# Row sums in a symmetric attention kernel: four of twelve steps folded aside instead of eight, and reductions allowed only in steps that turn nothing

## The chip, the cores and the metric

The kernel runs on one core of a Trainium2 chip. Its time is the device time of one execution in microseconds. TensorE (PE in the profile) multiplies matrices, VectorE (DVE), ScalarE (ACT) and GpSimd (POOL) work on tiles of 128 partitions, and SyncE (SP) issues most of the DMA transfers. Each engine has its own list of instructions, and semaphores make one engine wait for another.

## The reference, cut to what matters

The network has several layers on four images of 128 channels and 64x64 positions. The change touches one part of layer 2 only, attention in which queries, keys and values are all the same tensor `q`, with 16 heads of 8 numbers over L = 4096 positions:

```
qkv = _qz_ring(heads + rx_theta)
q = jnp.transpose(qkv, (0, 2, 1, 3))
scores = jnp.einsum('bhsd,bhtd->bhst', q, q) / np.sqrt(D)
attn = jax.nn.softmax(scores, axis=-1)
ctx = jnp.einsum('bhst,bhtd->bhsd', attn, q)
```

(The reference reshapes the four images of 4096 positions as its batch.) Queries and keys are the same, so the matrix of scores is symmetric: exp of the score of query s with key t is also that of query t with key s. The softmax is computed as a sum of exp times value, the numerator, divided by a sum of exp, the denominator.

## The kernel before

**Tiles.** For one head the 4096 queries are cut in four blocks `j` = 0 to 3 of 1024, and the keys in sixteen tiles `m` = 0 to 15 of 256. A step of the loop in line 1103 is one (head `h`, block `j`, key tile `m`). It makes 256 x 1024 scores on TensorE (lines 1119 to 1126, tile `score`), their exp on ScalarE in two instructions (line 1142, `p` = 0 and 1, tile `ex`, four buffers), and multiplies exp by values on TensorE into `ctx_ps` one step later (`weigh`, line 1041).

**Symmetry.** The kernel makes only the scores with `m // 4 >= j`. A step with `m // 4 > j` (the code calls it `behind`) is used a second time: VectorE turns its two halves into the tile `turned`, the first half in the same step (line 1148) and the second in the next step (line 1129, through `upright`). Four such steps fill one `turned` tile. Some steps later TensorE multiplies it by values into `acc_ps` (`turn`, line 995, eight turns a group), and VectorE copies or adds the finished group into `acc` (lines 1021 and 1023). Steps with `m // 4 == j` turn nothing.

**Row sums.** The denominator of the turned side is the sum of each row of `ex` over its 1024 queries. It is made in one of two ways, as `folded(j, m)` (line 1083) says:

- ScalarE accumulates it while it makes the exp (`accum_out` in line 1143), two instructions with an accumulator read each;
- or the step is "aside": GpSimd folds `ex` in two additions, 128x2048 values to 128x1024 (line 1090, `folded`) and to 128x512 (line 1091, `quarters`, six buffers), and VectorE reduces the quarters to two columns of `dacc` (line 1135). Line 1092 puts the reduction on the list `folds` with the step from which it is due.

**Order.** `pairs(j)` (line 968) gives the order of the key tiles in a block, and line 977 the blocks: block 0 of head h, block 3 of head h-1, block 1 and block 2 of head h. From head to head 40 steps repeat. I number them as places 0 to 39. Place by place the key tiles are

```
block 0, places  0-15: 4 5 6 0  7 8 9 1  10 11 12 2  13 14 15 3
block 3, places 16-19: 12 13 14 15      (of the head before)
block 1, places 20-31: 8 9 4  10 11 5  12 13 6  14 15 7
block 2, places 32-39: 12 8  13 9  14 10  15 11
```

and the steps that turn nothing are places 3, 7, 11, 15 to 19, 22, 25, 28, 31, 33, 35, 37 and 39. The lists of TensorE, VectorE and GpSimd stand in this order as written (`manual_schedule`, line 1256). Within a step VectorE's list is: the copy of a group that the step's turns have finished; the second transposition of the step before; the copy of `ctx_ps` at the end of a block (line 1072); the reductions that are due; the first transposition of this step. TensorE's list is: scores, turns (line 1127), `ctx_ps` products of the step before. A group may be turned from two steps after its last step on (`begun[...] < n - 1`).

With j = 0, 1, 2 the steps aside are, before the change, 8 of 12, 4 of 8 and 3 of 4, so 15 for each head.

Of the kernel before, what the change touches and what calls it, by code (L numbers as in the profile page):

```python
# [29 lines left out]
class Common:  # L30
# [57 lines left out]
    def mm(self, out, lhsT, rhs, start=True, stop=True):  # L88
        self.nc.tensor.matmul(out, lhsT, rhs, start=start, stop=stop)  # L89
# [685 lines left out]
def layer2_attention(K, xd, dpool, w):  # L775
# [6 lines left out]
    with ExitStack() as ctx:  # L782
# [126 lines left out]
        def attention(qt, dsum, big, work, pssc, psctx, psacc):  # L909
# [11 lines left out]
            def load(h, queues=(nc.sync, nc.sync)):  # L921

                out = []
                for keys in (True, False):
                    t = work.tile([P, L // 2], F32R, name="keys" if keys else "queries")
                    raw = t.bitcast(F32)
                    n = P if keys else CH
                    for p in range(2):  # L930
                        for c in range(2):
                            for k in range(4):
                                r = unit(p, c).start + HD * k
                                src = head_d[k // 2 if keys else k % 2, HD * h : HD * h + HD]
                                at = p if keys else c
                                queues[not keys].dma_start(  # L936
                                    out=raw[r : r + HD].rearrange("d (m s) -> d m s", s=n),
                                    in_=src.rearrange("d (m z s) -> d m z s", z=2, s=n)[:, :, at],
                                )
                    out.append(t)  # L940
                return out

            def rounded(t):

                nc.gpsimd.tensor_copy(t, t.bitcast(F32))  # L945
# [12 lines left out]
            def spread_values(v):  # L958
                t = work.tile([P, 4 * BT, 4, HD], F32, name="turned_v")
                nc.gpsimd.tensor_tensor(  # L960
                    t,
                    v.unsqueeze(2).to_broadcast([P, 4 * BT, 4, HD]),
                    quarter.unsqueeze(1).to_broadcast([P, 4 * BT, 4, HD]),
                    ALU.mult,
                )
                return t
# [63 lines left out]
            def turns(n, ready):  # L1030


                due = left = 0
                for g in groups:
                    left += BT - g[0]
                    due = max(due, -(-left // max(1, g[5] - n + 1)))
                for _ in range(min(max(due, 1), 3)):
                    if not groups or not ready(groups[0]) or turn():
                        return
# [41 lines left out]
            folds = []  # L1081

            def folded(j, m):

                return ((m - 4) % 3 < 2, m % 2 == 0, m % 4 < 3)[j]

            def fold(n, exs, at):
                hs = work.tile([P, 2, CH], F32, name="folded", bufs=1)
                qs = work.tile([P, 2, CH // 2], F32, name="quarters", bufs=6)
                nc.gpsimd.tensor_tensor(hs, exs[:, :, 0], exs[:, :, 1], ALU.add)  # L1090
                nc.gpsimd.tensor_tensor(qs, hs[:, :, 0 : CH // 2], hs[:, :, CH // 2 :], ALU.add)  # L1091
                folds.append((n + 5, qs, at))

# [7 lines left out]
            for n, (h, j, m) in enumerate(steps):  # L1103
                now[0] = n
                keys, queries = heads[h]
                if j in (1, 2) and h + 1 < NH:
                    at = n - begins[h, 1]
                    if at == 0:
                        heads[h + 1] = load(h + 1)
                    if at in (11, 15):  # L1110
                        rounded(heads[h + 1][at == 15])
                while waiting and n >= waiting[0][0]:
                    _, at, v = waiting.pop(0)
                    values[at] = spread_values(v)
                behind = m // 4 > j
                if n in ends:
                    turned = work.tile([P, BT, 2 * CH], F32, name="turned")
                    end = min(ends[n], last[h, m // 4])
                sps = [pssc.tile([P, 2, CH], F32, name="score") for p in range(2)]
                for p in range(2):  # L1120
                    for c in range(2):
                        mm(
                            sps[p][:, c, :],
                            keys[unit(p, c), m * P : (m + 1) * P],
                            queries[unit(p, c), j * CH : (j + 1) * CH],
                        )
                turns(n, lambda g: begun[id(g[4])] < n - 1)
                if upright is not None:
                    nc.vector.transpose(*upright)  # L1129
                    upright = None  # L1130
                if past is not None:
                    weigh(*past)
                while folds and folds[0][0] <= n:
                    _, qs, at = folds.pop(0)
                    nc.vector.tensor_reduce(at, qs, AX.X, ALU.add)  # L1135
                exs = work.tile([P, 2, 2, CH], F32, name="ex", bufs=4)
                aside = behind and folded(j, m)
                for p in range(2):
                    ex = exs[:, p]
                    t = 2 * m + p  # L1140
                    summed = behind and not aside
                    nc.scalar.activation(  # L1142
                        ex, sps[p], AF.Exp, scale=scale, accum_out=dacc[:, j, h, t : t + 1] if summed else None
                    )
                    if behind:
                        upright = turned[:, t % BT, :], ex.rearrange("p c s -> p (c s)")
                        if p == 0:
                            nc.vector.transpose(*upright)  # L1148
                if aside:
                    fold(n, exs, dacc[:, j, h, 2 * m : 2 * m + 2])  # L1150
                past = (h, j, m, exs)
                if behind and m % 4 == 3:
                    begun[id(turned)] = n
                    groups.append([0, h, j, m // 4, turned, end, None])
# [82 lines left out]
        for b in range(NB + 1):  # L1237
            with tc.tile_pool(name="l2_big", bufs=1) as big:
                with (
                    tc.tile_pool(name="l2_mid", bufs=2) as work,  # L1240
                    tc.tile_pool(name="l2_ps", bufs=8, space=PSUM) as psum,
                ):
                    parts = [feed_forward(b - 1, past, work, psum)] if b > 0 else []
                    if b < NB:
                        part, qt = prepare(b, big, work, psum)
                        parts.append(part)
                    run(*parts)
                if b == NB:
                    break
                past = keep.tile([P, NTT, NH], F32, name="dsum")  # L1250
                with (
                    tc.tile_pool(name="l2_work", bufs=2) as work,
                    tc.tile_pool(name="l2_pssc", bufs=3, space=PSUM) as pssc,
                    tc.tile_pool(name="l2_psctx", bufs=1, space=PSUM) as psctx,
                    tc.tile_pool(name="l2_psacc", bufs=1, space=PSUM) as psacc,
                    tc.manual_schedule(
                        engines={mybir.EngineType.PE, mybir.EngineType.DVE, mybir.EngineType.Pool}
                    ),
                ):
                    attention(qt, past, big, work, pssc, psctx, psacc)  # L1260
# [433 lines left out]
```

## Time and profile before

| what | value |
|---|---|
| runs, median (lowest to highest) | 11169.24 us (11165.61 to 11181.6) |
| profiled execution, its own time | 11175.99 us |
| its span on the core | 11174.1 us |
| attention, four images | 1369.6, 1370.4, 1367.5, 1370.3 us |
| one head inside an image (40 steps) | 85.3 us |
| PE, DVE, ACT, POOL busy over the span | 81%, 70%, 66%, 55% |
| exp, L1142 | 5120 of 1.031 us |
| first transposition, L1148 | 1536 of 1.232 us |
| second transposition, L1129 | 1536 of 1.208 us |
| reduction of quarters, L1135 | 960 of 0.648 us |
| fold and second fold, L1090 and L1091 | 960 of 2.387 us and 960 of 1.285 us |
| accumulator read of exp, L1142 | 1152 of 0.208 us |

Times are those of one profiled execution. A timeline has one row for each instruction or run of like instructions: its start in us from the start of the span, its length, engine, source line, what it writes and reads, how many; in square brackets the idle time of the engine just before it and the work that ended this idle time. TensorE's matrix multiplications all have line 89 (a helper), so they are told apart by tile. Lengths of neighbours on VectorE and ScalarE overlap by some hundredths of a microsecond, so what an instruction takes from its engine is read from start to start.

### The profile page before, as it was taken

Reading aid. Unit: us, or ns where it says so; the run is one execution under the profiler, and the core shown is the slowest. Engines: PE = TensorE matmul, PEld = TensorE weight load, DVE = VectorE, ACT = ScalarE, POOL = GpSimd, SP = SyncE. Lnnn points to the kernel's source line nnn. Section 1 sums busy time; section 2 is a strip of 40 time slices with the busy share of each in tenths; the row PEclk is TensorE's granted clock in tenths of the full one; section 3 lists DMA queues with packets and bytes.
Section 4 is the critical chain, followed back from the end, with each engine's and each line's share of the span. In section 5 each row is a group of like instructions: output and inputs, shape, how many; then the busy total and the mean of one; then the engine's idle time right before and its main releaser. Section 6 shows DMA issues by size and latency. Waiting matters only on the chain.

```text
span 11174.1 us, 183363 instructions
## 1 busy us (share of the span) xinstructions
PE 9093.3 (81%) x71376; PEld 3383.0 (30%) x71376; DVE 7817.5 (70%) x8718; ACT 7349.5 (66%) x9690; POOL 6136.5 (55%) x3631
## 2 busy tenths in 40 slices
PE   5777777778757999967999967999967999966767
PEld 2222223223122333322333322333322333323433
DVE  2688687687846788856888756878856888844564
ACT  2655454654527899947988947988946998842431
POOL 0466455455626777726777736777736777720000
PEclk8787878878778999978999979999978999978888
DMA  3322322322212221122221222221122221122004
GB/s 86 83 70 52 100 64 62 92 62 61 61 46 39 34 33 34 30 73 36 37 33 32 32 74 34 38 32 33 32 73 34 35 37 33 32 87 78 30 16 136
DMA packets 524324, 581.53 MB, mean 52 GB/s; under 512 B 106232, under 2 KB 329536, under 8 KB 520896
## 3 DMA queue, kind: packets, MB, share of 16 engines
q1 hardware_dynamic: 520896, 565.61, 22.4%
q8 instruction: 563, 9.22, 0.4%
q10 hardware_dynamic: 2560, 4.20, 0.3%
q14 instruction: 305, 2.50, 0.1%
HBM read 373.96 MB, written 76.55 MB: 40 GB/s over the span
## 4 chain that ended last, share of the span: by engine, by line
PE 35%; DVE 16%; DMA 8%; SPq 4%; ACT 3%; issue 2%; POOL 1%; DVEq 0%; ACTq 0%; POOLq 0%
PE ctx_ps L89 12%; PE acc_ps L89 9%; DVE turned L1129 5%; PE score L89 5%; DVE turned L1148 5%; SPq L936 4%; DMA queries<-head_d 3%; DMA keys<-head_d 2%; PE ln_var L89 2%; PE ln_xc L89 1%; PE hid_ps L89 1%; DMA w<-in_L_ffn_weight 1%; PE ffn_ps L89 1%; ACT ex L1142 1%; PE kv L89 1%
## 5 line engine op out<-in xcount | busy, mean ns | idle before, releaser
L1142 ACT ACTIVATE ex<-score 128x1024 f32<-128x1024 f32 x5120 | 4904.7, 1031 | 598.5 <-PE score L89 224.9
L1090 POOL TENSOR_TENSOR folded<-ex 128x1024 f32<-128x1024 f32 x960 | 2291.5, 2387 | 1173.3 <-ACT ex L1142 1141.8
L89 PE MATMUL ctx_ps<-ex,qt 128*32 128x512 f32 x20480 | 2722.5, 596 | 0.0
L1148 DVE STREAM_TRANSPOSE turned<-ex 128x1024 f32<-128x1024 f32 x1536 | 1892.0, 1232 | 596.5 <-ACT ex L1142 392.8
L89 PE MATMUL acc_ps<-turned,turned_v 128*32 128x256 f32 x24576 | 1828.5, 389 | 220.7 <-DVE turned L1129 219.0
L1129 DVE STREAM_TRANSPOSE turned<-ex 128x1024 f32<-128x1024 f32 x1536 | 1854.8, 1208 | 0.0
L89 PE MATMUL score<-queries,keys 32*128 32x512 f32 x10240 | 1360.2, 497 | 240.9 <-POOL queries L945 145.9
L641 DVE TENSOR_TENSOR_SCAN hs<-decay,carry,hs 128x512 f32<-128x512 f32 x1024 | 1247.8, 1263 | 151.6 <-ACT decay L640 142.3
L640 ACT ACTIVATE decay<-dt,a_neg 128x512 f32<-128x512 f32 x1024 | 699.9, 690 | 875.1 <-DVE hs L641 871.5
L1091 POOL TENSOR_TENSOR quarters<-folded 128x512 f32<-128x512 f32 x960 | 1233.8, 1285 | 75.3
L647 POOL TENSOR_TENSOR hs<-hs,c_sb 128x1024 f32<-128x1024 f32 x512 | 1201.7, 2368 | 48.1 <-DMA c_sb<-c_d 28.4
L89 PEld LDWEIGHTS score<-queries,keys 32*128 32x128 f32 x10240 | 523.4, 182 | 2300.9 <-issue 1656.8
L89 PEld LDWEIGHTS acc_ps<-turned,turned_v 128*32 128x32 f32 x24576 | 562.1, 108 | 938.9 <-issue 545.2
L89 PE MATMUL y_ps<-hs,pair 128*64 128x512 f32 x2048 | 654.5, 757 | 223.0 <-POOL hs L647 222.8
L89 PEld LDWEIGHTS ctx_ps<-ex,qt 128*32 128x32 f32 x20480 | 684.9, 110 | 462.2 <-DVE ctx L1072 53.2
L637 DVE TENSOR_TENSOR hs<-dtx,b_ps 128x2048 f32<-128x2048 f32 x256 | 581.4, 2271 | 318.9 <-PE b_ps L89 218.2
L644 POOL COPY carry<-hs 128x4 f32<-128x4 f32 x256 | 65.1, 254 | 1105.2 <-DVE hs L641 1090.8
L1135 DVE TENSOR_REDUCE dacc<-quarters 128x2 f32<-128x512 f32 x960 | 617.2, 648 | 0.0
L1072 DVE COPY ctx<-ctx_ps 128x512 f32<-128x512 f32 x256 | 177.1, 692 | 565.3 <-PE ctx_ps L89 565.3
L89 PE MATMUL ln_var<-ln_sq,mean 128*128 128x512 f32 x448 | 289.6, 732 | 219.0 <-ACT ln_sq L104 183.1
L89 PE MATMUL b_ps<-dbc,spread 32*128 32x512 f32 x512 | 341.6, 751 | 147.8 <-DVE hs L637 147.8
L960 POOL TENSOR_TENSOR turned_v<-v,quarter 128x1024 f32<-128x1024 f32 x192 | 458.9, 2391 | 0.0
(344 smaller groups left out, 9320.8 us busy)
## 6 DMA issues: line engine op xcount, KB each, us to landing
c_sb<-c_d SPq DMA_DIRECT2D x512, 128.0 KB
keys<-head_d SPq DMA_DIRECT2D x1024, 64.0 KB
queries<-head_d SPq DMA_DIRECT2D x960, 64.0 KB
dt<-dt SPq DMA_DIRECT2D x128, 256.0 KB
dtx<-dtx SPq DMA_DIRECT2D x128, 256.0 KB
w<-in_L_ffn_weight SPq DMA_DIRECT2D x32, 1024.0 KB
w<-in_L_ffn_weight SPq DMA_DIRECT2D x128, 256.0 KB
under<-xp SPq DMA_DIRECT2D x384, 66.0 KB
```

What stands on the lines that cost most here:

```text
L89: self.nc.tensor.matmul(out, lhsT, rhs, start=start, stop=stop)
L637: nc.vector.tensor_tensor(hs, dtx2, bb.unsqueeze(1).to_broadcast([P, NQ, CH]), ALU.mult)
L640: nc.scalar.activation(ex, dt2[:, q, :], AF.Exp, scale=a_neg[:, q, g : g + 1])
L641: nc.vector.tensor_tensor_scan(hs[:, q, :], ex, hs[:, q, :], carry[:, g, q : q + 1], ALU.mult, ALU.add)
L647: nc.gpsimd.tensor_tensor(at, at, cs.unsqueeze(1).to_broadcast([P, 2, CH]), ALU.mult)
L960: nc.gpsimd.tensor_tensor(t, v.unsqueeze(2).to_broadcast([P, 4 * BT, 4, HD]), quarter.unsqueeze(1).to_broadcast([P, 4 * BT, 4, HD]), ALU.mult,
L1090: nc.gpsimd.tensor_tensor(hs, exs[:, :, 0], exs[:, :, 1], ALU.add)
L1091: nc.gpsimd.tensor_tensor(qs, hs[:, :, 0 : CH // 2], hs[:, :, CH // 2 :], ALU.add)
L1129: nc.vector.transpose(*upright)
L1135: nc.vector.tensor_reduce(at, qs, AX.X, ALU.add)
L1142: nc.scalar.activation(ex, sps[p], AF.Exp, scale=scale, accum_out=dacc[:, j, h, t : t + 1] if summed else None)
L1148: nc.vector.transpose(*upright)
```

## The change

```diff
             def folded(j, m):
 
-                return ((m - 4) % 3 < 2, m % 2 == 0, m % 4 < 3)[j]
+                return ((m - 4) % 3 == 0, m % 2 == 0, m % 4 < 3)[j]
 
             def fold(n, exs, at):
...
-                folds.append((n + 5, qs, at))
+                folds.append((n + 3, qs, at))
...
-                while folds and folds[0][0] <= n:
+
+                while folds and (folds[0][0] <= n and not behind or len(folds) > 5):
                     _, qs, at = folds.pop(0)
                     nc.vector.tensor_reduce(at, qs, AX.X, ALU.add)
```

In block 0 the key tiles 4, 7, 10 and 13 stay aside; 5, 8, 11 and 14 get their row sums from ScalarE's accumulator instead. A head has 11 steps aside instead of 15, so the kernel has 704 instead of 960. A reduction is due three steps after its fold instead of five, but is given to VectorE only in a step that turns nothing, unless more than five are waiting.

Lines from 1133 on move down by one.

## The prediction

> **What bounds the kernel now.** I first read the busy times of one image's attention as a stretch of its own, since the change touches nothing else.
>
> ```profile
> core 0: us, PE busy (x) PEld busy (x) DVE busy (x) ACT busy (x) POOL busy (x), PEclk, DMA share, GB/s
> 5087.50:6457.90 1370.40, 1302.11 (x14569) 464.15 (x14569) 1101.20 (x1167) 1230.59 (x1568) 1046.06 (x558) 1.00 0.21 32
> ```
>
> TensorE is busy 1302 of 1370 us at a granted clock of 1.00, so it is the bound, and at most its idle 68 us per image can go. ScalarE follows with 1231 us. GpSimd, which the change relieves most, has 1046 us and room. Next I asked the waits of TensorE in one head of 40 steps (head 6 of the second image, 85.3 us):
>
> ```profile
> PE acc_ps L89 <- DVE turned L1129: 3.3, 5, 1.6
> PE score L89 <- ACT ex L1142: 0.9, 1, 0.9
> ```
>
> TensorE waits 3.3 us, five times, for a second transposition (L1129), and once 0.9 us for an exp. Its timeline puts the five at places 0, 6, 11, 26 and 32, with 0.17, 0.41, 1.55, 0.67 and 0.55 us: each time the first turn of a new group. The 0.9 us comes at place 39. Heads inside an image repeat this to some hundredths. The page's groups tell what stands in VectorE's list beside transpositions:
>
> ```profile
> L89 PE MATMUL acc_ps<-turned,turned_v 128*32 128x256 f32 x24576 | 1828.5, 389 | 220.7 <-DVE turned L1129 219.0
> ...
> L1135 DVE TENSOR_REDUCE dacc<-quarters 128x2 f32<-128x512 f32 x960 | 617.2, 648 | 0.0
> ```
>
> All such waits together are 219 us; the 960 reductions are 617 us of VectorE. So the question is which reductions stand ahead of which late transposition. That is read from VectorE's timeline before the longest wait:
>
> ```profile
> 5609.76 0.64 DVE L1135 TENSOR_REDUCE dacc<-quarters 128x2 f32<-128x512 f32 x1
> 5610.32 1.23 DVE L1148 STREAM_TRANSPOSE turned<-ex 128x1024 f32<-128x1024 f32 x1
> 5611.48 1.20 DVE L1129 STREAM_TRANSPOSE turned<-ex 128x1024 f32<-128x1024 f32 x1
> 5612.61 0.64 DVE L1135 TENSOR_REDUCE dacc<-quarters 128x2 f32<-128x512 f32 x1
> 5613.17 1.23 DVE L1148 STREAM_TRANSPOSE turned<-ex 128x1024 f32<-128x1024 f32 x1
> 5614.32 1.21 DVE L1129 STREAM_TRANSPOSE turned<-ex 128x1024 f32<-128x1024 f32 x1
> 5615.78 1.25 DVE L1148 STREAM_TRANSPOSE turned<-ex 128x1024 f32<-128x1024 f32 x1 [0.25 <-ACT ex L1142]
> 5618.00 0.42 DVE L1021 COPY acc<-acc_ps 128x256 f32<-128x256 f32 x1 [0.97 <-PE acc_ps L89]
> 5618.35 1.24 DVE L1129 STREAM_TRANSPOSE turned<-ex 128x1024 f32<-128x1024 f32 x1
> 5619.50 0.64 DVE L1135 TENSOR_REDUCE dacc<-quarters 128x2 f32<-128x512 f32 x1
> 5620.07 1.23 DVE L1148 STREAM_TRANSPOSE turned<-ex 128x1024 f32<-128x1024 f32 x1
> 5621.22 1.20 DVE L1129 STREAM_TRANSPOSE turned<-ex 128x1024 f32<-128x1024 f32 x1
> ```
>
> These are the transpositions of places 5, 6, 8 and 9. The last row ends at 5622.42, and TensorE's turn starts at 5622.48:
>
> ```profile
> 5620.16 0.77 PE L89 MATMUL score<-queries,keys 32*128 32x512 f32 x4
> 5622.48 0.64 PE L89 MATMUL acc_ps<-turned,turned_v 128*32 128x256 f32 x8 [1.55 <-DVE turned L1129]
> ```
>
> Elsewhere a turn starts 0.43 us after its scores; here 2.32 us. So 1.88 us are lost, of which the profile shows 1.55 as idle. Three reductions lie in this stretch, each 0.56 us from its start to the next.
>
> **What the Trainium skill says.** Perfetto Trace Analysis, section "Tensor Engine Instruction (MATMUL, LD_WEIGHTS)", says that VectorE, ScalarE and GpSimd are strict FIFOs. The trace agrees: the copy L1021 sat 0.97 us, and the transposition behind it with it, though its exp had ended at 5616.67. VectorE: DVE Perf Modes, section "Rules for kernel authors", advises restructuring when a reduction lies on a hot path; here it costs 0.56 us for 512 values a partition. ScalarE: Activation LUTs, section "What it computes", names the accumulator output but no price; the trace gives one below.
>
> **The change part by part.**
>
> *GpSimd loses folds.* Four a head, 256 in all, of 2.387 + 1.285 us: 940 us of its work. Value: nothing. Exps that reuse an `ex` buffer wait for the fold of four places earlier (places 4, 5, 8, 9, 12, 13, 16, 17), and those folds ended 1.4 us or more ahead of them. The casts of keys and queries keep their order, and no wait of TensorE inside a head is for them.
>
> *VectorE loses 256 reductions and the rest move.* 256 x 0.56 = 143 us leave its list. Only what stands ahead of a late transposition counts, so I go through the waits with the new list: of each head's eleven reductions one stands at each of places 3, 7, 11, 15, 25, 28, 31, 33, 35, 37 and 39, behind the second transposition of the step before.
>
> - Place 6, 0.41 us. From the copy of `ctx_ps` at 5599.19 to the transposition that ends at 5609.84 VectorE never idles, and one reduction lies between (5602.08). It goes to place 39 of the head before, but that of place 0's fold comes to place 3. One for one: 0.
> - Place 11, 1.55 us. The first reduction (5609.76) goes; the transpositions behind it start up to 0.5 us earlier. The second is replaced by that of place 7. But place 8's first transposition must wait for its exp (5615.75) and the copy L1021 for TensorE (5618.00): both clocks are TensorE's, so what was gained before them is absorbed. The third (5619.50) stands after them and goes. The two transpositions behind it have their exp ready (it ended at 5618.95), so they end 0.57 us earlier, at 5621.85, and so does TensorE's wait: **0.57**.
> - Places 26 and 32, 0.67 and 0.55 us. No reduction lies between the copy of `ctx_ps` or the ScalarE-bound transposition that begins either chain and its last transposition: 0.
> - Places 39 and 0, 0.86 and 0.17 us. ScalarE's exp of place 38 is late, and in both built programs it waits for TensorE's `ctx_ps` product of place 37. Untouched: 0.
>
> What is late next at place 11 is the same transposition, 1.31 us behind instead of 1.88.
>
> The first head of each image is different, since there no block 3 lies between blocks 0 and 1 to let VectorE catch up. Its timeline shows TensorE idle 1.54 us at place 11 as above, and then 0.82 us (turn at 5125.19) and 1.26 us (5138.58). Ahead of the first stand two more reductions (5119.04, 5121.89), ahead of the second another two (5130.08, 5132.93), and none in the new list. Two are 1.13 us, less what exps that follow TensorE, now itself earlier, hold back. My walk with the rows' starts gives 0.7 and 0.65. Sum for an image: 1.35.
>
> *ScalarE gains accumulations.* Four steps a head, two instructions each, 512 in all. An exp with accumulator takes 1.00 us to the next start (5630.19 less 5629.19), one without 0.92 (a row of two is 1.94 long, one alone 1.02), and the read, 0.208 us in its own row, overlaps the next exp. Price 0.08 to 0.10 each, 41 to 51 us in all; I take 0.10. If the whole read were exposed it would be 0.208, 106 us: the upper end. The lower end is zero, since more work on a FIFO can't gain. Value on the path: 0. What places 1, 5 and 9 lose, 0.2 us each, is covered by the idle 0.41, 0.55 and 0.31 us before the exps of places 2, 7 and 10. Place 13 is tightest: the exps of place 14 start 0.2 us later against TensorE, and the second half of place 15's scores reuses the buffer of the first of them. It ended at 5629.22, the scores start at 5629.51, so 0.29 us of cover shrink to about 0.1. If that is gone, it costs up to 0.2 a head, 13 us.
>
> *The new due time.* A reduction now comes three to five steps after its fold and VectorE waits there if GpSimd isn't done, with the next block's copies and transpositions queued behind it. At place 7 the quarters were ready at 5612.38 and VectorE comes at about 5614.5. At place 39, behind the cast of queries, they end at 5680.51 and VectorE comes at 5681.93. Both are in time: 0. `len(folds) > 5` never holds.
>
> **Sum.** 64 x 0.57 = 36.5; 4 x 1.35 = 5.4; together 42 us. Against the profiled execution, 11175.99 (span 11174.1 and 1.9 around it), that is 11134. The median of the runs is 6.75 lower, 11169.24, so I predict 11127 us. About 0.2%, 22 us, is what a measurement of this kernel can tell from no change.
>
> **The rivals.**
>
> *Absorbed.* The third reduction's place is taken up too, by the copy L1021 or an exp. For it: two of three reductions in the stretch go that way already. Against it: after 5618.35 the rows follow without a gap. Time 11169, within 10.
>
> *ScalarE comes onto the path (slower).* In block 0 it has eight accumulating steps of twelve. If its backlog isn't emptied between pairs of them (places 1-2, 5-6, 9-10, 13-14), exps come late, transpositions wait for them instead of for reductions, and the 0.57 isn't had. Price 4 x 2 x 0.10 = 0.8 us a head, 51 in all: 11220. It decides from the point where the exps at place 9 come 1.6 us later (transposition at 5620.65 against their new end of about 5619.05). For it: ScalarE is second in busy time. Against it: gaps of 0.31 to 1.28 us before places 7, 8, 9, 10 and 12.
>
> *More is freed.* If place 6's chain also loses its reduction, because VectorE gets to place 3 early enough, 64 x 0.41 = 26 us more: 11101. The FIFO walk speaks against it.
>
> **How the numbers follow.** The forecast has 0.74, its own range 11112 to 11142 (up to 13 us less for the tight score, 15 more for head 0 and neighbours). Absorbed 0.12, slower 0.05, more freed 0.09. Two tenths may be left out, so the range takes part of the freed case and some shortfall: 11098 to 11152. Faster by over 0.2% is the forecast and the freed case less a little: 0.81. Within: 0.14. Slower: 0.05.
>
> **What would show it.** In the new profile TensorE's wait at place 11 should be near 1.0 us instead of 1.55, those at places 6, 26, 32, 39 and 0 as they are, a head near 84.7 us instead of 85.3, the waits on L1129 near 178 us instead of 219, and no reduction between two transpositions of steps 8 and 9. ScalarE should have 1664 accumulator reads. Wrong: idle before exps gone in block 0, or VectorE waiting for quarters.

## The result and the profile after

| what | before | after |
|---|---|---|
| runs, median | 11169.24 us | 11122.35 us |
| runs, lowest to highest | 11165.61 to 11181.6 us | 11118.96 to 11132.05 us |
| profiled execution, its own time | 11175.99 us | 11123.57 us |
| its span | 11174.1 us | 11121.7 us |
| attention, four images | 1369.6, 1370.3, 1367.5, 1370.3 us | 1357.3, 1356.5, 1356.6, 1356.6 us |
| one head inside an image | 85.30 us | 84.71 us |

The median fell by 46.9 us; the ratio of after to before is 0.9956, its interval 0.9941 to 0.997. The forecast was 42 us less. The two profiled executions lie 52.4 us apart, of which 50.7 are in the attention (5477.7 less 5427.0 us, the four images together).

First the busy times of the same stretch, one image's attention, in the profile after. The columns are those of the prediction's first fence.

```profile
core 0: us, PE busy (x) PEld busy (x) DVE busy (x) ACT busy (x) POOL busy (x), PEclk, DMA share, GB/s
5076.40:6432.90 1356.50, 1299.70 (x14568) 463.98 (x14569) 1062.13 (x1103) 1240.51 (x1696) 812.00 (x430) 1.00 0.20 33
```

GpSimd has lost 234 us of work in this image and VectorE 39, ScalarE has gained 10, and the stretch is 13.9 us shorter. None of these three differences by itself is the gain, as the experiments show; TensorE's idle time fell from 68 to 57 us. Next the waits of TensorE in the same head (head 6 of the second image), in the profile after:

```profile
PE acc_ps L89 <- DVE turned L1129: 2.8, 5, 1.0
PE score L89 <- ACT ex L1143: 0.9, 1, 0.9
```

There are still five waits for the second transposition, and they are shorter by the difference of the longest alone: 1.6 us has become 1.0. In the timeline they stand at the same places 0, 6, 11, 26 and 32, now with 0.18, 0.40, 0.96, 0.67 and 0.55 us. VectorE's timeline ahead of the longest, in the profile after, for the same transpositions of places 5, 6, 8 and 9 as before:

```profile
5590.65 1.20 DVE L1149 STREAM_TRANSPOSE turned<-ex 128x1024 f32<-128x1024 f32 x1
5591.78 1.21 DVE L1129 STREAM_TRANSPOSE turned<-ex 128x1024 f32<-128x1024 f32 x1
5592.90 1.21 DVE L1149 STREAM_TRANSPOSE turned<-ex 128x1024 f32<-128x1024 f32 x1
5594.03 1.21 DVE L1129 STREAM_TRANSPOSE turned<-ex 128x1024 f32<-128x1024 f32 x1
5595.15 0.65 DVE L1136 TENSOR_REDUCE dacc<-quarters 128x2 f32<-128x512 f32 x1
5596.67 1.25 DVE L1149 STREAM_TRANSPOSE turned<-ex 128x1024 f32<-128x1024 f32 x1 [0.87 <-ACT ex L1143]
5598.90 0.42 DVE L1021 COPY acc<-acc_ps 128x256 f32<-128x256 f32 x1 [0.98 <-PE acc_ps L89]
5599.24 1.23 DVE L1129 STREAM_TRANSPOSE turned<-ex 128x1024 f32<-128x1024 f32 x1
5600.40 1.20 DVE L1149 STREAM_TRANSPOSE turned<-ex 128x1024 f32<-128x1024 f32 x1
5601.52 1.20 DVE L1129 STREAM_TRANSPOSE turned<-ex 128x1024 f32<-128x1024 f32 x1
```

The reductions are one where three were. The one at 5595.15 sits ahead of the wait for the exp of place 8, and that wait has grown from 0.25 to 0.87 us: VectorE now reaches the exp earlier and stands still. The copy L1021 waits 0.98 us for TensorE, as before. Only behind this copy has something gone that counts: no reduction lies between the last three rows. TensorE's rows in the profile after:

```profile
5601.05 0.77 PE L89 MATMUL score<-queries,keys 32*128 32x512 f32 x4
5602.78 0.64 PE L89 MATMUL acc_ps<-turned,turned_v 128*32 128x256 f32 x8 [0.96 <-DVE turned L1129]
```

The turn starts 1.73 us after its scores; before it was 2.32. The page's groups say the same of the whole kernel:

```profile
L89 PE MATMUL acc_ps<-turned,turned_v 128*32 128x256 f32 x24576 | 1826.2, 388 | 176.4 <-DVE turned L1129 173.5
...
L1136 DVE TENSOR_REDUCE dacc<-quarters 128x2 f32<-128x512 f32 x704 | 453.5, 644 | 0.0
```

The waits for the second transposition fell from 219.0 to 173.5 us, by 45.5.

### The profile page after: what moved, and what is told of

The parts are those of the page before. It is cut to its first block, busy times and chain, and to the rows that moved or that the text cites. A ratio compares the mean times of both kernels' runs of the same rounds, so it can differ in the third digit from the quotient of the medians.

```text
span 11121.7 us, 182595 instructions
## 1 busy us (share of the span) xinstructions
PE 9097.9 (82%) x71376; PEld 3388.7 (30%) x71376; DVE 7663.7 (69%) x8462; ACT 7388.9 (66%) x10202; POOL 5198.2 (47%) x3119
## 5 line engine op out<-in xcount | busy, mean ns | idle before, releaser
L1090 POOL TENSOR_TENSOR folded<-ex 128x1024 f32<-128x1024 f32 x704 | 1679.1, 2385 | 2077.9 <-ACT ex L1143 2054.8
L89 PE MATMUL acc_ps<-turned,turned_v 128*32 128x256 f32 x24576 | 1826.2, 388 | 176.4 <-DVE turned L1129 173.5
L1091 POOL TENSOR_TENSOR quarters<-folded 128x512 f32<-128x512 f32 x704 | 905.2, 1286 | 55.2
L1136 DVE TENSOR_REDUCE dacc<-quarters 128x2 f32<-128x512 f32 x704 | 453.5, 644 | 0.0
```

## The experiments

The theory on record was: the third reduction of place 11 is the gain, by its place in VectorE's list, and fewer folds give nothing. The rivals were that the gain comes from GpSimd's or VectorE's lighter load, and that ScalarE's added accumulations cost something. Each ratio is to the kernel before, run on the same chip; for each kernel the time of a head inside an image in its trace is given too, since it repeats to some hundredths of a us, while what lies outside the attention ranged from 5690.6 to 5713.1 us over the twelve profiled executions though no kernel changes it. The first three edits stand in the kernel before, all the others in the kernel after.

### One part alone: fewer folds

```diff
-                return ((m - 4) % 3 < 2, m % 2 == 0, m % 4 < 3)[j]
+                return ((m - 4) % 3 == 0, m % 2 == 0, m % 4 < 3)[j]
```

> The kernel before with only the new choice of steps aside (4 of 12 in block 0); reductions stay due five steps after their fold, in any step. Theory: what counts is the one reduction between the transpositions of places 8 and 9, and with folds at places 0, 4, 8 and 12 the reductions come at places 5, 9, 13 and 17, so that one stays. TensorE's idle time at place 11 stays 1.55 us, a head inside an image stays 85.3 us, and the time falls only by the first heads, some 4 us, to about 11165 us, although GpSimd loses 940 us of work and VectorE 143 us. Since the long wait stays, the short stretches of half TensorE clock at place 11 of the first heads stay too. Rival (the relief of GpSimd and VectorE as such brings the gain): about 11122 us and a head of 84.7 us. Rival (accumulations cost ScalarE time on the path): above 11190 us.

Measured: 11170.21 us (13 runs), ratio 1.0001, interval 0.9993 to 1.0009. A head takes 85.31 us, as before. VectorE's timeline in this kernel, from the end of place 5's transpositions on, and TensorE's turn:

```profile
5622.08 1.20 DVE L1129 STREAM_TRANSPOSE turned<-ex 128x1024 f32<-128x1024 f32 x1
5623.20 1.20 DVE L1148 STREAM_TRANSPOSE turned<-ex 128x1024 f32<-128x1024 f32 x1
5624.33 1.20 DVE L1129 STREAM_TRANSPOSE turned<-ex 128x1024 f32<-128x1024 f32 x1
5626.38 1.25 DVE L1148 STREAM_TRANSPOSE turned<-ex 128x1024 f32<-128x1024 f32 x1 [0.85 <-ACT ex L1142]
5628.61 0.42 DVE L1021 COPY acc<-acc_ps 128x256 f32<-128x256 f32 x1 [0.98 <-PE acc_ps L89]
5628.95 1.23 DVE L1129 STREAM_TRANSPOSE turned<-ex 128x1024 f32<-128x1024 f32 x1
5630.11 0.64 DVE L1135 TENSOR_REDUCE dacc<-quarters 128x2 f32<-128x512 f32 x1
```
```profile
5633.09 0.64 PE L89 MATMUL acc_ps<-turned,turned_v 128*32 128x256 f32 x8 [1.55 <-DVE turned L1129]
```

The reduction that stood between places 5 and 6 is gone, and the wait for the exp takes all of it: 0.85 us instead of 0.25. The reduction behind the copy is still there, and TensorE still waits 1.55 us. So 256 folds, 256 reductions and 512 accumulations, moved from two engines to a third, are worth nothing to a head inside an image. Only the first head of each image gains: in the third image it takes 78.43 us instead of 79.58, because two of the four reductions ahead of its second and third late turn are gone (these waits are 0.68 and 0.65 us, before they were 1.27 and 1.25). Over four images that is 4.6 us, too little for the medians to show.

### The other part alone: the rule

```diff
-                folds.append((n + 5, qs, at))
+                folds.append((n + 3, qs, at))
...
-                while folds and folds[0][0] <= n:
+                while folds and (folds[0][0] <= n and not behind or len(folds) > 5):
```

> The kernel before with only the new rule for reductions (due three steps after the fold, in steps that turn nothing); block 0 keeps 8 of 12 steps aside. Theory: no reduction lies between the transpositions of places 8 and 9 any more, and the two reductions that now come together at place 7 are absorbed by the wait for the exp of place 8. So nearly the whole gain of the change: a head of 84.7 us, TensorE idle about 1.0 us at place 11, time 11120 to 11135 us. Rival (relief of GpSimd and VectorE): no gain, 11169 us. Rival (reductions wait for GpSimd's quarters, now due two steps earlier with the full number of folds): VectorE idle until quarters in its list, slower than the changed kernel by more than 15 us.

Measured: 11120.6 us, ratio 0.9952, interval 0.9939 to 0.9964; a head 84.70 us, the images 1356.5 to 1356.9 us. That is the whole change's gain, with all fifteen folds of a head kept.

### One reduction of each head moved by one step

```diff
-                while folds and folds[0][0] <= n:
+                while folds and folds[0][0] <= n and (j, m) != (0, 11):
```

> The kernel before with one edit: no reduction is given to VectorE in block 0's step of key tile 11 (place 9), so that the one that stood between the transpositions of places 8 and 9 comes one step later, behind place 9's second transposition. The same folds, the same number of reductions, the same accumulations. Theory: this one reduction is the whole 0.57 us a head: a head of 84.7 us, idle at place 11 about 1.0 us, time 36 us below before from the heads and up to 7 more if the stretches of half clock go, 11126 to 11136 us. Rival (the gain is spread over all the reductions that left): 5 us or less.

Step (0, 11) is place 9. Its reduction goes to the next step. VectorE's and TensorE's timelines of this kernel:

```profile
5617.08 1.24 DVE L1129 STREAM_TRANSPOSE turned<-ex 128x1024 f32<-128x1024 f32 x1
5618.24 1.20 DVE L1148 STREAM_TRANSPOSE turned<-ex 128x1024 f32<-128x1024 f32 x1
5619.37 1.20 DVE L1129 STREAM_TRANSPOSE turned<-ex 128x1024 f32<-128x1024 f32 x1
5620.49 1.24 DVE L1135 TENSOR_REDUCE dacc<-quarters 128x2 f32<-128x512 f32 x2
```
```profile
5620.62 0.64 PE L89 MATMUL acc_ps<-turned,turned_v 128*32 128x256 f32 x8 [0.95 <-DVE turned L1129]
```

Measured: 11134.41 us, ratio 0.9966, interval 0.9952 to 0.9979. No reduction has been taken out, yet the wait is 0.95 us and a head 84.70 us, that of the kernel after. In the traces its attention is 5.8 us longer than that of the kernel after, all of it in the first head of each image: 79.0 to 79.3 us instead of 77.5 to 78.1, with the waits of 1.27 and 1.25 us there untouched.

### A reduction put back at this place, once and twice

```diff
                     nc.vector.tensor_reduce(at, qs, AX.X, ALU.add)
+                    again = at, qs
+                if (j, m) == (0, 11):
+                    for _ in range(1):
+                        nc.vector.tensor_reduce(*again, AX.X, ALU.add)
```

The kernel after has no reduction in place 9's step. Here the reduction given last, that of place 7, is made again there, into the same columns. In the second kernel the range is 2.

> The changed kernel with one needless reduction put back where the kernel before had one: in the step of place 9, between the second transposition of place 8 and the first of place 9 (it repeats the reduction given to VectorE at place 7; GpSimd's folds and ScalarE's accumulations stay as changed). Theory: this alone takes the gain of the heads back: idle at place 11 1.55 us again, a head 85.3 us, and the 3.4 us stretches of half TensorE clock at place 11 come back in some of the first two heads of the images (4 or 5 of 8, as in the kernel before). Time 36 to 43 us above the changed kernel, 11158 to 11165 us. Rival: the gain stays for the most part, and the half clock doesn't come back, since GpSimd and VectorE as a whole are relieved.

> The same with two needless reductions in that place. Theory: idle at place 11 2.1 us, a head 85.85 us, 73 us above the changed kernel from the heads; if the length of that idle time is what brings the half clock, it comes at least as often as with one, in 5 or more of the first two heads of the images: time 11195 to 11210 us. Rival for the clock (it is chance, not the idle time): no more than before.

Measured: once 11168.42 us (12 runs), ratio 1.0001, interval 0.9992 to 1.0009; a head 85.30 us, the wait at place 11 1.55 us. One reduction at this place is the change backwards. Twice: 11261.78 us, ratio 1.0084, interval 1.0068 to 1.0101. This is more than the 11195 to 11210 us expected, and only in small part by the price of the reductions: a head takes 86.02 us, where 85.85 were expected, or 87.6, and the second kind has a stretch in which TensorE's granted clock is half. The windows of this kernel, one image and then one such stretch, and TensorE's rows in it:

```profile
5104.10:6486.00 1381.90, 1304.17 (x14490) 463.50 (x14493) 1082.36 (x1134) 1235.91 (x1690) 811.92 (x430) 0.99 0.21 32
5385.00:5389.50 4.50, 4.50 (x36) 1.15 (x28) 3.27 (x4) 1.77 (x2) 0.00 (x0) 0.62 0.02 4
```
```profile
5384.79 0.64 PE L89 MATMUL acc_ps<-turned,turned_v 128*32 128x256 f32 x8 [2.27 <-DVE turned L1129]
5385.24 1.67 PE L89 MATMUL ctx_ps<-ex,qt 128*32 128x512 f32 x8
5386.84 0.80 PE L89 MATMUL score<-queries,keys 32*128 32x512 f32 x4
```

Right behind an idle time of 2.27 us the eight products into `ctx_ps` take 1.67 us instead of 1.04, at a PEclk of 0.62 over the window. It lasts 3.4 us each time and happens in 26 of the 64 heads. Against the once-more kernel the attention is 82 us longer (5552.3 less 5470.2): 64 x 0.72 = 46 us of idle time, and 23 stretches more of 1.57 us each, 36 us. In the last section I come back to it.

### No fold in block 0 at all

```diff
-                return ((m - 4) % 3 == 0, m % 2 == 0, m % 4 < 3)[j]
+                return (False, m % 2 == 0, m % 4 < 3)[j]
```

> The changed kernel with no step of block 0 aside: all its 12 turning steps accumulate on ScalarE, another 4 a head. It asks how near ScalarE is to the path. Theory: ScalarE has room for it, and the reduction at place 3 goes with its fold, so that the chain before place 6 is one reduction shorter: idle there falls from 0.38 us to near 0, a head to 84.3 us, time about 26 us below the changed kernel, 11090 to 11105 us. Rival (ScalarE comes onto the path): 0.4 us more exp time a head shows, the idle at place 6 is replaced by waits for exps, head 84.7 to 85.1 us, time 11122 to 11150 us.

Measured: 11119.78 us, ratio 0.9951, interval 0.9937 to 0.9964; a head 84.59 us, 0.12 less than after. This fell between the two theories. The wait at place 6 is gone, since its chain has lost its last reduction: from place 6's scores to place 7's it is 2.37 us instead of 2.78. But more than half comes back through ScalarE. The step before place 6's scores takes 1.85 us instead of 1.71 and that before place 15's 1.98 instead of 1.86, 0.26 in all. TensorE's rows of this kernel ahead of place 15's scores, with those scores last, and ScalarE's row of the first exp of place 14:

```profile
5604.17 1.16 PE L89 MATMUL ctx_ps<-ex,qt 128*32 128x512 f32 x8
5605.26 0.52 PE L89 MATMUL score<-queries,keys 32*128 32x512 f32 x4
```
```profile
5604.10 1.04 ACT L1143 ACTIVATE ex<-score 128x1024 f32<-128x1024 f32 x1
```

The products take 1.16 us instead of 1.04, without an idle time that the profile shows. The scores reuse the buffer of that exp, which ends at 5605.14, and start 0.12 us later. In the kernel after it is 0.13 us, but the step there is still 1.86 us long: the cover that the prediction called the tightest is just used up with the eight accumulating steps of the change, and with twelve the scores follow the exp. Place 6's scores follow the exp of place 5 in the same way, 0.12 us behind its end.

### The reduction taken out of place 6's chain

```diff
-                folds.append((n + 3, qs, at))
+                folds.append((n + (3 if steps[n][1] == 2 else 4), qs, at))
```

The fold of place 0 is then reduced at place 7 instead of 3.

> The changed kernel with the reductions of blocks 0 and 1 due four steps after their fold instead of three (block 2 keeps three), so that none stands at place 3 and the chain of VectorE from the copy of ctx_ps to place 6's turn is one reduction shorter; it comes to place 7, where a wait for an exp absorbs it. Theory (the wait at place 6 remained because its reduction was replaced one for one): idle at place 6 falls from 0.38 us to 0.1 or less, nothing else changes, a head 84.3 us, time 20 to 26 us below the changed kernel, 11096 to 11103 us. Rival (the chain is bound by exps or the copy of acc, not by the reduction): no change, 11122 us.

Measured: 11113.08 us, ratio 0.9941, interval 0.9924 to 0.9957; a head 84.40 us. The wait at place 6 went from 0.40 to 0.08 us, with all folds and accumulations in place. So nearly all of the 0.41 us of place 6 was one reduction, which the change replaced one for one. The attention in this trace is 17.6 us shorter than in that of the kernel after, a little less than the 20 to 26 us expected.

### The second transposition ahead of the finished group's copy

```diff
-                turns(n, lambda g: begun[id(g[4])] < n - 1)
                 if upright is not None:
...
                     upright = None
+                turns(n, lambda g: begun[id(g[4])] < n - 1)
```

> The changed kernel with VectorE's second transposition of the step before put ahead of the step's turns, and so ahead of the copy of a finished group (L1021, L1023) in VectorE's list. Theory (what is left of the waits at places 11, 26, 32 and 0 is that copy, waiting for TensorE at the head of the queue or taking 0.3 us ahead of the last transposition): idle at place 11 falls from 0.95 us to 0.2 or less, those at places 26, 32 and 0 by 0.3 us each, a head by 1.7 to 2.0 us to 82.7 to 83.0 us, time 109 to 128 us below the changed kernel, 10994 to 11013 us. Rival (VectorE's own load bounds place 11, or the copies that now come later hold TensorE up): less than 40 us.

Measured: 11067.9 us, ratio 0.9905, interval 0.989 to 0.992; a head 83.81 us, 0.90 less than after, half of what was expected. TensorE's waits in the same head of this kernel:

```profile
PE score L89 <- ACT ex L1143: 0.9, 1, 0.9
PE acc_ps L89 <- DVE acc L1021: 0.6, 1, 0.6
PE acc_ps L89 <- DVE acc L1023: 0.5, 1, 0.5
PE acc_ps L89 <- DVE turned L1128: 0.4, 1, 0.4
```

The wait at place 11 is gone, all 0.96 us of it: there the copy L1021, which waits for TensorE, no longer stands ahead of the late transposition. Those of places 26 and 32 are as long as before but for another instruction: now TensorE waits for the copy itself, which has moved behind the transposition. `acc_ps` is one tile with two halves, and the first turn of a group now starts right behind the copy of the group before, 0.15 us after its end at place 26, although that copy reads the other half. Two separate tiles weren't tried, so it isn't shown that they would end this wait.

### Five `ex` buffers

```diff
-                qs = work.tile([P, 2, CH // 2], F32, name="quarters", bufs=6)
+                qs = work.tile([P, 2, CH // 2], F32, name="quarters", bufs=3)
...
-                exs = work.tile([P, 2, 2, CH], F32, name="ex", bufs=4)
+                exs = work.tile([P, 2, 2, CH], F32, name="ex", bufs=5)
```

> The changed kernel with five ex buffers instead of four (and three of quarters instead of six, which makes the room). With four, the exp of place 38 was given the buffer of place 37 and so waits for TensorE's product of place 37; with five it waits for its own scores only. Theory: the wait at place 39 (1.49 us lost, 0.86 of it shown as idle) goes, and place 0's with it, since its transposition was late for the same exp: a head 1.5 to 1.8 us shorter, 82.9 to 83.2 us, time 96 to 115 us below the changed kernel, 11007 to 11026 us. Rival (the exp was late for ScalarE's own backlog): no change.

Measured: 11048.83 us, ratio 0.989, interval 0.9876 to 0.9905; a head 83.34 us, 1.37 less. Of the waits in the head one line is left:

```profile
PE acc_ps L89 <- DVE turned L1129: 2.7, 5, 1.0
```

The wait for an exp at place 39 is gone, and from the exps of place 37 to those of place 38 it is 1.87 us instead of 3.32. So the exp of place 38 had waited for a buffer that the `ctx_ps` product of place 37 still read. The gain is a little under the 1.5 us expected because place 0 now waits 0.28 us instead of 0.18 for its transposition. The first and the last head of each image gain nothing, so the attention in this trace is 76.1 us shorter than in that of the kernel after, not the 96 to 115 us expected.

### The last three together

```diff
+                folds.append((n + (3 if steps[n][1] == 2 else 4), qs, at))
...
-                turns(n, lambda g: begun[id(g[4])] < n - 1)
...
+                turns(n, lambda g: begun[id(g[4])] < n - 1)
...
+                exs = work.tile([P, 2, 2, CH], F32, name="ex", bufs=5)
```

> The three together: reductions due four steps after the fold in blocks 0 and 1, second transposition ahead of the copies, five ex buffers. Theory: the gains add, 0.4 + 1.7 to 2.0 + 1.5, the one at place 0 counted once: a head of 80.8 to 81.1 us, time 230 to 250 us below the changed kernel, 10872 to 10892 us. Rival (ScalarE, then near 78 us of work a head, becomes the bound): a head above 81.5 us, with waits for exps in its place.

Measured: 10973.7 us, ratio 0.9819, interval 0.9805 to 0.9834. It beats both kernels. A head takes 82.01 us, 2.70 less than after, where the three alone sum to 0.31 + 0.90 + 1.37 = 2.58. What is left of the waits in the head:

```profile
PE acc_ps L89 <- DVE acc L1021: 0.6, 1, 0.6
PE acc_ps L89 <- DVE acc L1023: 0.5, 1, 0.5
```

The 80.8 to 81.1 us expected were not had. These two waits for copies, 1.1 us, are as large as the difference. The rival had put the head above 81.5 us too, but with waits for exps, and there are none.

## Why the prediction was right, point by point

**Place 11.** Right in place and nearly in size: 0.57 us predicted, 1.55 to 0.96 measured, 0.59 for a head. That the first two reductions would be absorbed and only the third count was the step that carried the forecast. Fewer folds alone shows the absorbing (the wait for the exp grows from 0.25 to 0.85 us, TensorE's stays), and one moved reduction shows the counting (same number of reductions, the whole 0.6 us). Putting it back undoes the gain to 0.01 us a head.

**Places 6, 26, 32, 39 and 0.** All predicted at nothing; measured 0.41 to 0.40, 0.67 to 0.67, 0.55 to 0.55, 0.86 to 0.87 and 0.17 to 0.18 us. The reasons held for the two that were put to a test: place 6 by the later due time, place 39 by the fifth buffer. Place 0 was given the same reason as 39, and this part is not borne out: with five buffers the exp of place 38 is early, and place 0 still waits for its transposition, longer than before. For places 26 and 32 the prediction only said that no reduction lies there; the copies behind are what the sixth experiment added.

**GpSimd and VectorE relieved.** Predicted at nothing inside an image for both; the rule with all folds kept and the change with four fewer a head give the same head, 84.70 and 84.71 us.

**ScalarE.** Predicted as hidden, with a cover of 0.1 us left at place 15. It held: 0.01 us a head between those two kernels, and 0.13 us measured at place 15. That place 15 is near the limit was right, since the kernel without folds in block 0 pays 0.12 us there. But it was not the tightest spot. In the kernel before, the second half of place 6's scores already starts 0.10 us behind the end of the exp whose buffer it reuses, against 0.29 us at place 15; the prediction did not look there, and the kernel without folds in block 0 pays 0.14 us before place 6. That the change itself paid nothing at place 6 was luck. The count of accumulator reads, from the view of the tile `ex` in the profile after:

```profile
L1143 ACT ACTIVATION_READ_ACCUMULATOR ex<-score x1664: 188/203/276, 3405.0 to 9766.2; 128x1 f32 x185
```

**The due time.** No wait of VectorE for quarters is among its waits in the head after. Right.

**The first head of each image.** Predicted 0.57 + 1.35 = 1.92 us. In the third image, whose clock is full throughout, it went from 79.58 to 77.50 us, 2.08. The second and third wait fell there from 1.27 and 1.25 us to 0.40 and 0.64. The second, 0.82 us, had been read in the second image, where a stretch of half clock had slowed TensorE shortly before it, so its full size and its gain of 0.86 us (0.7 predicted) were not seen.

**What was missed.** Heads 2 to 15 of the four images became 33.0 us shorter, 31.9 were predicted. Heads 0 and 1 became 17.7 us shorter, 10.0 were predicted. This term of the sum was too small. The trace of the kernel before has what the sum leaves out, five stretches of half clock in the first two heads of an image. Here are its windows with two of them, and TensorE's rows of the first:

```profile
5109.00:5118.00 9.00, 7.46 (x68) 2.32 (x60) 7.17 (x9) 5.80 (x8) 5.08 (x4) 0.81 0.36 50
5190.00:5200.00 10.00, 8.45 (x76) 2.59 (x72) 8.64 (x10) 6.92 (x10) 8.15 (x6) 0.83 0.06 16
```
```profile
5112.12 1.07 PE L89 MATMUL acc_ps<-turned,turned_v 128*32 128x256 f32 x16 [1.54 <-DVE turned L1129]
5113.01 1.86 PE L89 MATMUL ctx_ps<-ex,qt 128*32 128x512 f32 x8
```

The PEclk of these windows is 0.81 and 0.83, where the whole image shows 1.00 in two decimals, and that is why I took the clock as full. A window of head 0 alone (5087.54 to 5168.25) already shows 0.95. The products behind the wait at place 11 take 1.86 us instead of 1.04. Three such stretches lie in heads 1 (86.92 us, and 85.49 in the third image, which has none) and two in heads 0 (80.7 against 79.6): 3 x 1.43 + 2 x 1.1 = 6.5 us. In the kernel after there are none, so 6.5 of the 7.7 us missed are theirs. The rest is 0.1 to 0.2 us for each of the eight heads. Outside the attention the profiled executions differ by 1.7 us more, which nothing explains.

By the medians the forecast is 4.7 us too high, within what the interval of the ratio leaves open (34 to 66 us less). In the two profiled executions most of what it lacked is the half clock; how often that came in the other runs isn't known. Of the rivals, "absorbed" and "ScalarE onto the path" are refuted by the experiments named. "More is freed" didn't come by itself, but its mechanism and nearly its size (0.31 of 0.41 us) were there to be had by a later due time.

## What to carry to other kernels

Follow the list of an in-order engine backwards from the late instruction to the last one that waits for another engine: what is taken out ahead of that point is absorbed, and what is taken out behind it counts in full, so moving one reduction of 0.56 us in each head brought more than taking out four folds and four reductions elsewhere. Look for who else is near before you take out a wait: here the copies behind the transposition took over most of two waits. Read the granted clock in windows of some us around an idle time, not over a stage.

## What the runs showed of the hardware that was not expected

TensorE's clock can fall to half for 3.4 us right behind an idle time of 1.55 us, and whether it does depends on when that idle time ends. Counted over the 64 heads, by the idle time at place 11, leaving out the start of each image:

| kernel | idle at place 11 | stretches of half clock |
|---|---|---|
| after, and the seven others with this wait or less | up to 0.96 us | 0 |
| before; fewer folds; once more | 1.55 us | 5; 4; 3 |
| twice more | 2.27 us | 26 |

Each cost a head 1.1 to 1.6 us. With 1.55 us it struck almost only heads 0 and 1 of an image (once head 6); with 2.27 us it came at intervals of one to three heads.

Why it strikes one head and not the next, with the same idle time in both, can be read from the times of the clock changes, which each trace keeps beside the instructions. In all twelve traces every change of the granted clock lies on one grid of 3.4133 us, to 0.001 us. The five stretches of the kernel before, for example, begin at 3505.42, 5113.10, 5195.02, 8485.47 and 8567.39 us, which is 471, 24, 964 and 24 steps from one to the next. The heads are counted here by the time from the end of the idle time to the next point of this grid, where the half clock begins if it comes:

| kernel | idle at place 11 | to the next grid point | heads | with half clock |
|---|---|---|---|---|
| before; fewer folds; once more | 1.55 us | 1.05 us or less (once 0.06 us past the point) | 12 | 12 |
| | | 1.19 to 3.20 us | 180 | 0 |
| twice more | 2.27 us | 1.34 us or less | 26 | 26 |
| | | 1.36 to 2.51 us | 38 | 0 |
| the six with a wait of 0.96 us | 0.96 us | 0.00 to 3.41 us | 384 | 0 |

So the length decides whether an idle time at this place can bring the half clock at all: 0.96 us never did, wherever it ended, and 1.55 us did. Where it ends on the grid decides whether it does, and with 2.27 us the range is not much wider than with 1.55. The counts of 3 to 5 and of 26 differ mainly because of the length of a head. A head of 85.30 us is 25 grid steps (85.33 us) less 0.03, so from head to head the idle time nearly keeps its place on the grid, and a stretch in head 1 moved it out of the range for the rest of the image. A head of 86.02 us is 0.69 us longer than 25 steps, so the idle time runs into the range again and again. What the throttle counts, and what length between 0.96 and 1.55 us is enough, stay open.
